# A graph convolution on one core: transposes two groups ahead, and a new order of ScalarE's work

## The chip, the cores and the metric

The kernel runs on one core of a Trainium2 chip. The core has five engines, each with a queue of its own that is worked off in order: TensorE (PE) for matmuls and transposes, VectorE (DVE), ScalarE (ACT), GpSimd (POOL) and SyncE (SP), of which the last two mostly issue DMAs here. Engines wait for each other by semaphores. The metric is the device time of one execution in microseconds (us).

## The reference

One layer of a graph network: 12,500 nodes and 200,000 edges with 64 values each, the edges sorted by their target `dst`.

```python
nodes = x[edge_index].reshape(E, -1)                        # rows of src and dst, side by side
gates = ssp(edge_attr @ We1 + be1) @ We2 + be2              # ssp(x) = softplus(x) - log 2
gates = gates * (1 - sigmoid(5 * (edge_weight - 3.5)))
h     = ssp(nodes @ Wn1 + bn1) @ Wn2 + bn2
sum_  = zeros_like(x).at[dst].add(h * gates)                # messages summed by target
new   = x + ssp(sum_ @ Ws1 + bs1) @ Ws2 + bs2
out   = layernorm(x + new)
```

## The kernel before

**Groups.** The edges are worked in 391 groups of 512 (0 to 390). A group is cut into K = 4 slots of 128 edges. Since the edges are sorted, the targets of half a group lie in a window of W = 42 neighbouring nodes.

**What one group needs, by function.** `gather` (L204) issues on POOL one indirect DMA a slot, which fetches the rows of `src` into a buffer `xg`; the `xg` buffers form a ring of AHEAD + BEHIND. `onehot` (L277, DVE) writes beside these rows which of the 42 targets of the window each edge has. `transposes` (L283, PE) turns the four slots, rows and onehots together, into the PSUM tile `tx`; `xcopy` (L291, ACT) copies that to `xT`. The first layer is made in the PSUM tile `z`: `layer1_bias` (L296), `layer1_edge` (L301) and `layer1_node` (L308), which multiplies `xT` by `wns`: the first 64 rows of `wns` are the weights for `src`, its last 42 the window's rows of a table (nodes times the second half of Wn1, made earlier), which `load` brings by DMA on SP (L216 the edges' values, L224 the window's rows). Softplus is `exps` (L322, ACT), `logs` (L325, ACT) and `softplus` (L330, DVE). The second layer is `layer2_bias` (L347), `layer2_edge` (L354) and `layer2_node` (L359) into `gh`. `hcut` (L368) and `message` (L372) on DVE form the messages, `scatter` (L376, PE) sums them by target into a corner of another group's `z` (it multiplies them by the onehots in `xg`, and is thus the last reader of that buffer), and `window` (L396, DVE) adds that to `sums` at the window's place. The matmuls of L334 are fillers whose result is overwritten.

**Slots made of columns.** For 70 groups one slot isn't gathered from memory: its edges' rows are copied as columns from a copy of x in SBUF, `xh`. That is `columns` (L259): 16 copies on ACT and 8 on DVE in every iteration from 8 on. Their addresses are read into the engine's registers by `read_columns`. Such groups have three gathers and a memset (L202), and `layer1_node` adds two matmuls (L311) for the slot.

**Chunks.** The table is made in 98 chunks of 128 nodes, seven ahead of the loop and one in each of the iterations 0 to 90: `chunk` (L646, PE, into the same `z` as the scatter's sums; it reads x from the storage of `sums`), `keep_chunk` (L649, ACT, to an SBUF tile; every seventh time a DMA writes seven chunks out) and `clear` (L538, DVE).

**Node blocks.** As soon as the sums of 512 nodes are complete, the last layer and the layernorm for them are spread in parts over some iterations (L415 to L475).

**The order is written out by hand.** Python runs the loop for i from −1 to 388; each engine executes its instructions in the order of the program text, and the waits follow from the buffers. In iteration i before the change, cut to what bears on it:

```python
at(gather, i + AHEAD, range(K), [("transposes", i)] if i < BEHIND else ())
layer1_bias(i + 1); layer2_bias(i); scatter(i - 2)
transposes(i + 1); xcopy(i + 1); columns(i, ACT)
layer1_edge(i + 1); chunk(c) or filler; layer1_node(i + 1)
exps(i + 1); logs(i + 1)
keep_chunk(c)                        # c only for i = 0 .. 90
read_columns(i + 1, ACT)
window(i - 2); clear(c)
layer2(i); hcut(i); message(i); softplus(i + 1)
onehot(i + 3); columns(i, DVE)
```

So ACT works copy, columns, exponential, logarithm, chunk, addresses. PE has first layer, second layer, scatter and transposes of different groups in turn. The PSUM tiles `z`, `gh` and `tx` have two buffers each.

Of the kernel before, what the change touches and what calls it, by code (L numbers as in the profile page):

```python
# [31 lines left out]
PIECES = 3  # L32
NB = 512
K = 4
AHEAD = 3
CHUNKS = 7
HEAD = 64
LOADS = 5
SPREADS = 5
PREPARE = 5  # L40
BEHIND = 5
CLOSE = 12


# [60 lines left out]
def gnn_resnorm_kernel(ctx: ExitStack, tc: tile.TileContext, a: dict, out: bass.AP, E: int):  # L105
# [45 lines left out]
    packed, at = {}, 0  # L151
# [94 lines left out]
    def columns(i, queue, pool):  # L246

        count = min(COLUMNS[queue], columns_left(i, queue))
        for j in range(count):
            m, r = divmod(columns_done[queue] + j, P)  # L250
            slot = own[queue][m]
            if r == 0:
                column_tiles[slot] = pool.tile([P, P], F32, name=f"column{queue}", bufs=2)
                side_tiles[slot] = pool.tile([P, P], I32, name=f"side{queue}", bufs=2)
                at = slots.index(slot)
                nc.sync.dma_start(side_tiles[slot], a["sides"][at : at + 1, :].rearrange("o p -> (o p)")
                                  .partition_broadcast(P))
            copy = nc.vector.tensor_copy if queue == 0 else nc.scalar.copy
            copy(column_tiles[slot].bitcast(U8)[:, 4 * r : 4 * r + 4], xh[:, bass.ds(column_at[queue][j] - xh_at, 4)])  # L259
            if r == P - 1:  # L260
                whole.append(slot)
        columns_done[queue] += max(count, 0)
# [17 lines left out]
    def transposes(g, *needs):  # L280
        tx = tx_tile()[:DW].rearrange("f (k e) -> f k e", k=K)
        for k in range(K):
            ins = nc.tensor.transpose(tx[:, k, :], xgs[g][:, k, :DW], ident)  # L283
            if k == 0:
                behind(ins, *needs)
        note(("transposes", g), ins)
        xTs[g] = tx

    def xcopy(g):
        xT = work.tile([DW, K, P], F32, name="xT", bufs=3)  # L290
        note(("xcopy", g), nc.scalar.copy(xT, xTs[g]))  # L291
        xTs[g] = xT.rearrange("f (t h) e -> f h t e", h=2)
# [26 lines left out]
    def exps(g, part=every):  # L319
        if part.start == 0:  # L320
            us[g] = work.tile([P, 3 * HE], F32, name="u")
        nc.scalar.activation(us[g][:, part], z_of(g)[:, part], AF.Exp)  # L322
# [163 lines left out]
    with tc.manual_schedule():  # L486
# [28 lines left out]

        for g in range(AHEAD):
            gather(g)
# [99 lines left out]
        def highest():  # L617
            high = prep.tile([P, NR], F32, name="high")
            nc.vector.tensor_reduce(high, dst_h, AX.X, OP.max)
            nc.vector.tensor_sub(high, high, low)  # L620
            nc.vector.tensor_scalar(high, high, float(1 - W), None, OP.add)
            early = prep.tile([P, NR], F32, name="early")
            nc.vector.tensor_sub(early, least, low)
            nc.vector.tensor_max(high, high, early)
            span = t["span"] = prep.tile([P, 1], F32, name="span")
            nc.vector.tensor_reduce(span, high, AX.X, OP.max)
# [40 lines left out]
        with tc.tile_pool(name="finish", bufs=1) as finish:  # L667
            blocks = list(zip(node_blocks(N), block_steps(N, NG)))
            last = NG - 1
            parts, begun, complete, rest = {}, None, 0, []  # L670

            def at(f, g, *more):
                if 0 <= g < NG:
                    f(g, *more)

            def behind_by(i):
                close = last - CLOSE
                return [g for g in ([i - 2] if i <= close else []) + ([i - 1] if i >= close else []) if g >= 0]

            for g in range(LOADS - 1):  # L680
                load(g)
            for g in range(2):
                onehot(g)
            lowest(1, NR)
            everywhere(1, NR)
            clear(0, CHUNKS)
            highest()
            for i in range(-1, last - 1):
                now = parts.pop(i, [])
                early = [part for part in now if part.tensor]  # L690
                at(load, i + LOADS)
                if i >= 0:
                    at(gather, i + AHEAD, range(K), [("transposes", i)] if i < BEHIND else ())
                layer1_bias(i + 1)
                at(layer2_bias, i)
                for n, g in enumerate(behind_by(i)):
                    scatter(g, zs[i + 1][:, 1, HE + 2 * n * W : HE + 2 * (n + 1) * W])
                transposes(i + 1, ("load", i + 1), ("gather", i + 1), ("onehot", i + 1))
                xcopy(i + 1)
                columns(i, 1, finish)  # L700
                layer1_edge(i + 1)
                c = chunk_of(i, NCH)
                if c is None:
                    busy_before_node(i + 1)
                else:
                    beside_sums = zs[i + 1][:, 1, HE + 2 * W : HE + 2 * W + P]
                    chunk(c, beside_sums)
                layer1_node(i + 1)
                exps(i + 1)
                logs(i + 1)  # L710
                if c is not None:
                    keep_chunk(c, beside_sums)
                read_columns(i + 1, 1)
                for g in behind_by(i):
                    window(g)
                if c is not None:
                    clear(c, c + 1)
                at(busy_before_layer2, i)
                at(layer2, i)
                for part in early:  # L720
                    part.tensor(tx_tile())
                at(hcut, i)
                at(message, i)
                softplus(i + 1)
                for part in early:
                    part.others()
                at(onehot, i + 3)
                read_columns(i, 0)
                columns(i, 0, finish)
                choose(finish)  # L730
                for part in now:
                    if not part.tensor:
                        part.others()
                for action in beside.get(i, []):
                    action()
                complete = i
                if blocks and complete >= blocks[0][1] - PREPARE and not begun:
                    begun = node_block(*blocks[0][0], finish)
                    begun.pop(0).others()
                if blocks and complete >= blocks[0][1]:  # L740
                    steps = next(steps for steps in BLOCK_STEPS if i + steps[-1] < last - 1)
                    for n, part in zip(steps, begun):
                        parts.setdefault(i + n, []).append(part)
                    rest = begun[len(steps) :]
                    blocks.pop(0)
                    begun = None
            assert len(blocks) == 1 and begun and not parts


            begun.pop(2).others()  # L750
            transposes(last, ("load", last), ("gather", last), ("onehot", last))
            xcopy(last)
            layer1_bias(last)
            layer2_bias(last - 1)
            scatter(last - 2, zs[last][:, 1, HE : HE + 2 * W])
            layer1_edge(last)
            layer1_node(last)
            for some in (edge, node):
                exps(last, some)
                logs(last, some)  # L760
            square, variance, root, scale, store = (part.others for part in rest)
            square()
            window(last - 2)
            for g in range(last - 1, last + 1):
                if g not in window_at:
                    window_bases(g)
            layer2(last - 1)
            layer2_bias(last)
            softplus(last, edge)
            layer2_edge(last)  # L770
            softplus(last, node)
            layer2_node(last)
            hcut(last - 1)
            message(last - 1)
            scatter(last - 1, tx_tile()[:, : 2 * W])
            variance()
            root()
            hcut(last)
            message(last)
            scatter(last, tx_tile()[:, : 2 * W])  # L780
            window(last - 1)
            window(last)
            hidden, clamp = begun.pop(0)
            hidden(gh_tile())
            scale()
            clamp()
            store()
            for part in begun:
                node_part(part)
# [162 lines left out]
```

## Time and profile before

| what | us |
|---|---|
| median of 3 runs | 2394.47 (2393.62 to 2402.24) |
| the profiled execution: its time | 2389.88 |
| its span (first to last instruction) | 2388.1 |
| PE busy | 1970.5 (83%) |
| ACT busy | 1511.2 (63%) |
| POOL busy | 1417.0 (59%) |
| DVE busy | 1293.9 (54%) |

The mean granted clock of PE is 0.981. In the lines of the profile that follow, L308 is line 308 of the kernel. A line of the timeline gives start, duration, engine, line, operation, what it writes and reads, and in brackets how long the engine had been idle before it and what ended that. A line of the groups gives busy time, mean ns of one, and idle time with its releasers. Ends of matmuls are modelled. "issue" stands for idle time that no wait in the profile explains.

### The profile page before, as it was taken

What the parts mean: (1) busy time and instruction counts of PE and PEld (TensorE: products, weight loads), DVE (VectorE), ACT (ScalarE), POOL (GpSimd) and SP (SyncE); (2) the same over time, 40 slices, a digit from 0 to 9 for tenths busy, and PEclk for the clock granted to TensorE, in tenths of its full rate; (3) what the DMA queues carried; (4) which work ended last, traced back from release to release, by engine and by line L of the source; (5) the groups of instructions that cost most, each with busy time, mean ns of one, the idle gap of its engine ahead of it and who ended that gap; (6) DMA issues with size and microseconds to landing.
All of it is one profiled execution on the core that took longest, in us unless ns stands there. A gap on an engine that the chain in (4) does not pass through costs nothing.

```text
span 2388.1 us, 48209 instructions
## 1 busy us (share of the span) xinstructions
PE 1970.5 (83%) x12897; PEld 1656.7 (69%) x12897; DVE 1293.9 (54%) x5966; ACT 1511.2 (63%) x7412; POOL 1417.0 (59%) x1497
## 2 busy tenths in 40 slices
PE   6788888888888888888888888888888888888877
PEld 4666677767776776677677667766777767777765
DVE  4355555555555555555555555555555555555544
ACT  3466666666666666666666666666666666666653
POOL 5665665666666666666666666665665666666650
PEclk9799999999999999999999999999999999999988
DMA  6332232322222222222222222222222222222220
GB/s 185 85 91 68 56 75 56 77 61 71 54 57 56 53 59 54 57 56 62 53 59 55 57 58 55 59 59 54 58 58 56 59 57 60 63 57 58 59 50 14
DMA packets 159679, 148.63 MB, mean 62 GB/s; under 512 B 40564, under 2 KB 108949, under 8 KB 159274
## 3 DMA queue, kind: packets, MB, share of 16 engines
q1 hardware_dynamic: 111194, 94.97, 14.4%
q0 software_dynamic: 47776, 49.02, 10.8%
q8 instruction: 109, 1.79, 0.3%
q14 instruction: 166, 1.36, 0.2%
q10 hardware_dynamic: 434, 1.50, 0.2%
HBM read 135.70 MB, written 9.62 MB: 61 GB/s over the span
## 4 chain that ended last, share of the span: by engine, by line
PE 80%; issue 13%; ACT 3%; DVE 2%; another core or an unknown queue 1%; DMA 0%; DVEq 0%; ACTq 0%
PE z L308 18%; PE gh L359 13%; PE z L376 10%; PE tx L283 10%; PE gh L354 7%; PE z L301 6%; PE gh L334 4%; PE gh L347 3%; PE z L296 3%; PE z L334 2%; ACT xT L291 2%; PE tx L415 1%; PE tx L446 1%; PE z L311 1%
## 5 line engine op out<-in xcount | busy, mean ns | idle before, releaser
L204 POOL DMA_INDIRECT xg<-in_x,src_i x1493 | 1416.8, 949 | 919.3 <-PE tx L283 488.8
L308 PE MATMUL z<-xT,wns 106*128 106x256 f32 x1564 | 459.7, 412 | 359.9 <-issue 285.9
L291 ACT COPY xT<-tx 106x512 f32<-106x512 f32 x391 | 229.1, 586 | 779.3 <-PE tx L283 751.1
L259 ACT COPY column<-xh 128x4 uint8 x6016 | 608.7, 193 | 0.0
L308 PEld LDWEIGHTS z<-xT,wns 106*128 106x128 f32 x1564 | 267.8, 193 | 452.4 <-issue 337.7
L368 DVE TENSOR_TENSOR h<-gh,cut 128x256 f32<-128x256 f32 x391 | 165.9, 424 | 747.9 <-PE tx L283 632.2
L359 PE MATMUL gh<-consts,s 128*128 128x64 f32 x3128 | 396.0, 270 | 0.0
L359 PEld LDWEIGHTS gh<-consts,s 128*128 128x128 f32 x3128 | 385.0, 194 | 0.1
L325 ACT ACTIVATE u<-u,one 128x768 f32<-128x768 f32 x392 | 365.8, 933 | 13.4 <-ACT u L322 0.5
L330 DVE SCALAR_TENSOR_TENSOR s<-u,z 128x768 f32<-128x768 f32 x392 | 368.7, 941 | 0.4 <-issue 0.4
L322 ACT ACTIVATE u<-z 128x768 f32<-128x768 f32 x392 | 314.7, 803 | 43.4 <-PE z L308 19.0
L396 DVE TENSOR_TENSOR sums<-sums,z 64x42 f32 x778 | 152.4, 196 | 291.3 <-issue 207.4
L376 PEld LDWEIGHTS z<-xg,msg 128*128 128x128 f32 x1556 | 205.0, 192 | 140.6 <-issue 121.3
L376 PE MATMUL z<-xg,msg 128*128 128x84 f32 x1556 | 265.1, 293 | 15.3 <-DVE msg L372 15.3
L259 DVE COPY column<-xh 128x4 uint8 x2944 | 246.5, 219 | 0.4 <-issue 0.4
L354 PE MATMUL gh<-consts,s 128*128 128x128 f32 x1564 | 243.3, 279 | 1.3 <-DVE s L330 0.8
L283 PE MATMUL tx<-consts,xg 128*106 128x128 f32 x1564 | 238.1, 276 | 0.0
L301 PE MATMUL z<-eT,consts 128*128 128x256 f32 x782 | 237.3, 386 | 0.0
L354 PEld LDWEIGHTS gh<-consts,s 128*128 128x128 f32 x1564 | 210.0, 195 | 2.0 <-DVE s L330 1.1
L283 PEld LDWEIGHTS tx<-consts,xg 128*106 128x106 f32 x1564 | 182.5, 142 | 0.9 <-issue 0.9
L372 DVE TENSOR_TENSOR msg<-gh,h 128x256 f32<-128x256 f32 x391 | 165.8, 424 | 13.4
L334 PEld LDWEIGHTS gh<-consts 128*128 128x128 f32 x778 | 149.5, 195 | 20.5 <-issue 0.3
(109 smaller groups left out, 1456.2 us busy)
## 6 DMA issues: line engine op xcount, KB each, us to landing
eT<-in_eT SPq DMA_DIRECT2D x195, 256.0 KB
xg<-in_x,src_i POOLq DMA_INDIRECT x1493
wns<-table SPq DMA_DIRECT2D x782, 21.0 KB
table<-tb SPq DMA_DIRECT2D x14, 448.0 KB
side<-in_sides SPq DMA_DIRECT2D x70, 64.0 KB
y<-in_x SPq DMA_DIRECT2D x24, 128.0 KB
out<-y SPq DMA_DIRECT2D x24, 128.0 KB
xh<-in_xh SPq DMA_DIRECT2D x2, 781.5 KB
```

The costliest lines, as they stand in the source:

```text
L204: behind(note(("gather", g), nc.gpsimd.indirect_dma_start(out=xg[:, k, :D], out_offset=None, in_=x, in_offset=bass.IndirectOffsetOnAxis(ap ...
L259: copy(column_tiles[slot].bitcast(U8)[:, 4 * r : 4 * r + 4], xh[:, bass.ds(column_at[queue][j] - xh_at, 4)])
L283: ins = nc.tensor.transpose(tx[:, k, :], xgs[g][:, k, :DW], ident)
L301: nc.tensor.matmul(zs[g][:, 0, :HE], we1.rearrange("a h d -> a (h d)"), eTs[g], start=False, stop=True, skip_group_check=True)
L308: nc.tensor.matmul(zn, wns[:, g % REST, h, :], xTs[g][:, h], start=True, stop=not chosen, skip_group_check=True)
L322: nc.scalar.activation(us[g][:, part], z_of(g)[:, part], AF.Exp)
L325: nc.scalar.activation(us[g][:, part], us[g][:, part], AF.Ln, bias=one)
L330: nc.vector.scalar_tensor_tensor(ss[g].rearrange("p i t e -> p (i t e)")[:, part], us[g][:, part], BIG, z_of(g)[:, part], OP.min, OP.max)
L334: nc.tensor.matmul(z, we1.rearrange("a h d -> a (h d)"), ident, start=True, stop=True, skip_group_check=True)
L354: nc.tensor.matmul(v[:, 0, t], ss[g][:, 0, t, :], we2, start=False, stop=False, skip_group_check=True)
L359: nc.tensor.matmul(ghs[g][:, 1, 2 * t + h, :], ss[g][:, 1 + h, t, :], wn2, start=False, stop=h == 1 and t == 1, skip_group_check=True)
L376: ins = nc.tensor.matmul(sc, msgs[g][:, 2 * t : 2 * t + 2, :].rearrange("p h f -> p (h f)"), xgs[g][:, 2 * t : 2 * t + 2, D:DW], start=t = ...
```

## The change

`transposes` and `xcopy` of group i + 2 are issued in iteration i, where those of i + 1 were. Transposes of group 0 and their copy come ahead of the loop, those of the last group go from the epilogue into the loop. For this the onehots are made one group earlier too, and AHEAD is 4 and BEHIND 4 (3 and 5 before). On ACT the copy goes behind the exponential, and the load of the addresses and the columns go behind the logarithm; `keep_chunk` comes behind them. ACT's order is then exponential, copy, logarithm, addresses, columns, chunk.

```diff
-AHEAD = 3
+AHEAD = 4
...
-BEHIND = 5
+BEHIND = 4
...
-            for g in range(2):
+            for g in range(3):
                 onehot(g)
...
             highest()
+            transposes(0, ("gather", 0), ("onehot", 0))
+            xcopy(0)
             for i in range(-1, last - 1):
...
-                    at(gather, i + AHEAD, range(K), [("transposes", i)] if i < BEHIND else ())
+                    at(gather, i + AHEAD, range(K), [("transposes", i + 1)] if i < BEHIND else ())
                 layer1_bias(i + 1)
                 at(layer2_bias, i)
                 for n, g in enumerate(behind_by(i)):
                     scatter(g, zs[i + 1][:, 1, HE + 2 * n * W : HE + 2 * (n + 1) * W])
-                transposes(i + 1, ("load", i + 1), ("gather", i + 1), ("onehot", i + 1))
-                xcopy(i + 1)
-                columns(i, 1, finish)
+                transposes(i + 2, ("load", i + 1), ("gather", i + 2), ("onehot", i + 2))
                 layer1_edge(i + 1)
...
                 layer1_node(i + 1)
                 exps(i + 1)
+                xcopy(i + 2)
                 logs(i + 1)
+                read_columns(i, 1)
+                columns(i, 1, finish)
                 if c is not None:
                     keep_chunk(c, beside_sums)
-                read_columns(i + 1, 1)
                 for g in behind_by(i):
                     window(g)
...
-                at(onehot, i + 3)
+                at(onehot, i + 4)
...
-            transposes(last, ("load", last), ("gather", last), ("onehot", last))
-            xcopy(last)
-            layer1_bias(last)
+            layer1_bias(last, ("load", last))
```

## The prediction

> **What bounds the kernel now.** I read the page's first part (shares), its fifth part (groups and what ended their idle time), then the timeline of one iteration, because the shares name no bound: no engine is full.
>
> ```profile
> PE 1970.5 (83%) x12897; PEld 1656.7 (69%) x12897; DVE 1293.9 (54%) x5966; ACT 1511.2 (63%) x7412; POOL 1417.0 (59%) x1497
> L204 POOL DMA_INDIRECT xg<-in_x,src_i x1493 | 1416.8, 949 | 919.3 <-PE tx L283 488.8
> L308 PE MATMUL z<-xT,wns 106*128 106x256 f32 x1564 | 459.7, 412 | 359.9 <-issue 285.9
> L291 ACT COPY xT<-tx 106x512 f32<-106x512 f32 x391 | 229.1, 586 | 779.3 <-PE tx L283 751.1
> ```
>
> The tempting reading: PE waits 359.9 us ahead of L308 for the copied transposes, and the change makes that copy a group earlier. The timeline says what ends that wait. Here is an iteration with four gathers, then one with three (start, duration, work, idle before it and its releaser; one gather of each is left out).
>
> ```profile
> 1203.69 0.94 POOL L204 DMA_INDIRECT xg<-in_x,src_i  x1 [1.41 <-PE tx L283]
> ...
> 1205.35 0.61 PE L354 MATMUL gh<-consts,s 128*128 128x128 f32 x4
> ...
> 1205.79 1.00 PE L359 MATMUL gh<-consts,s 128*128 128x64 f32 x8
> 1206.19 0.94 POOL L204 DMA_INDIRECT xg<-in_x,src_i  x1 [0.30 <-issue]
> ...
> 1207.15 0.68 PE L376 MATMUL z<-xg,msg 128*128 128x84 f32 x4
> 1207.44 0.94 POOL L204 DMA_INDIRECT xg<-in_x,src_i  x1 [0.30 <-issue]
> ...
> 1208.53 0.39 PE L334 MATMUL z<-consts 128*128 128x128 f32 x2
> 1209.56 0.42 DVE L368 TENSOR_TENSOR h<-gh,cut 128x256 f32<-128x256 f32 x1 [2.79 <-PE tx L283]
> 1209.69 0.59 ACT L291 COPY xT<-tx 106x512 f32<-106x512 f32 x1 [2.40 <-PE tx L283]
> 1209.87 0.94 POOL L204 DMA_INDIRECT xg<-in_x,src_i  x1 [1.49 <-PE tx L283]
> 1210.02 0.42 DVE L372 TENSOR_TENSOR msg<-gh,h 128x256 f32<-128x256 f32 x1
> ...
> 1210.33 1.13 PE L308 MATMUL z<-xT,wns 106*128 106x256 f32 x4 [1.41 <-ACT xT L291]
> 1210.36 0.94 DVE L330 SCALAR_TENSOR_TENSOR s<-u,z 128x768 f32<-128x768 f32 x1
> ...
> 1212.37 0.94 POOL L204 DMA_INDIRECT xg<-in_x,src_i  x1 [0.30 <-issue]
> ...
> 1214.35 0.42 DVE L368 TENSOR_TENSOR h<-gh,cut 128x256 f32<-128x256 f32 x1 [1.41 <-PE z L376]
> ...
> 1214.66 0.94 POOL L204 DMA_INDIRECT xg<-in_x,src_i  x1 [1.35 <-PE tx L283]
> ```
>
> L359, whose result h needs, ends at 1206.79, yet h starts at 1209.56. Then h, the copy and POOL's next train of gathers all start within 0.31 us. That moment is 1209.56 − 1207.44 = 2.12 us after the last gather's start; in the short iteration it is 1214.35 − 1212.37 = 1.98. So while POOL runs its train, what PE has finished becomes visible only about 2.05 us after the train's last gather. Then POOL, which waits on L376 for a free xg buffer, starts the next train. A step from gather to gather is 1.25 (1206.19 to 1207.44). A period is three such steps, 2.12 and 0.31: 6.18 with four gathers (1203.69 to 1209.87), and with one step less 4.79 (1209.87 to 1214.66). The train and PE are in lockstep, and PE's wait for xT is what is left over. Behind the kernel's last gather h starts 0.04 us after L359 ends (2341.77), which speaks for POOL as the cause:
>
> ```profile
> 2335.56 0.95 POOL L204 DMA_INDIRECT xg<-in_x,src_i  x1 [0.30 <-issue]
> ...
> 2339.13 1.13 PE L308 MATMUL z<-xT,wns 106*128 106x256 f32 x4
> 2340.30 0.81 ACT L322 ACTIVATE u<-z 128x768 f32<-128x768 f32 x1 [1.22 <-PE z L308]
> 2340.77 1.00 PE L359 MATMUL gh<-consts,s 128*128 128x64 f32 x8
> 2341.14 0.93 ACT L325 ACTIVATE u<-u,one 128x768 f32<-128x768 f32 x1
> 2341.81 0.42 DVE L368 TENSOR_TENSOR h<-gh,cut 128x256 f32<-128x256 f32 x1 [0.26 <-PE gh L359]
> ```
>
> Why the trace holds PE's results back I can't say; that it will hold them in the changed kernel too is my main assumption.
>
> **The change, part by part.**
>
> *Transposes and copy one group earlier.* No instruction is added: four L283 and one L291 per group as before. What ends: L308 no longer waits for L291, 1.41 us in the iteration above. What is late next: L354, which waits for softplus, behind message, behind h, behind the held L359. From h's release that path is the same before and after: softplus (L330), for which L354 waits, ends at 1211.30, 1.74 us behind it. Nothing in it reads xT, and POOL's train waits on L376, not on L308. So L308 moves into the hole and PE stands the same time ahead of L354. Value in the steady part: 0. From the other side, if the wait for xT does set the pace, PE goes to the 4.79 of the short iteration; that is the first rival.
>
> *Rings and order.* The xg ring keeps 4 + 4 = 8 buffers, so gather g waits for scatter g − 8 as before: POOL's queue is the same, with four gathers more ahead of the loop. Onehots are made three ahead: one more in the prologue, none more in all; transposes of i + 2 wait for a onehot made two iterations earlier: 0. SP's loads aren't moved. At the end the last group's transposes and copy leave its path. They already stood ahead of its bias there, so what goes is at most one L291, 0.59, and PE's transposes, under the 0.70 between L376's end (1207.83) and L334 (1208.53), which holds L301 too; I take −1 (0 to −1.3).
>
> *ScalarE's new order, groups with no chunk.* Per iteration: exponential, copy, logarithm, load of addresses, columns. The spacings are 0.84 (2340.30 to 2341.14), 0.62, 0.93, 0.19 and 1.55 by the rows here and next, 4.13 in sum, under even the short period of 4.79. Window sums (L396) still wait for the exponential alone. Cost: 0.
>
> ```profile
> 484.20 1.62 ACT L259 COPY column<-xh 128x4 uint8 x16
> 485.75 0.81 ACT L322 ACTIVATE u<-z 128x768 f32<-128x768 f32 x1
> 1200.25 0.93 ACT L325 ACTIVATE u<-u,one 128x768 f32<-128x768 f32 x1
> 1201.38 0.42 ACT L454 ACTIVATE y<-y 128x256 f32<-128x256 f32 x1 [0.19 <-issue]
> ```
>
> The columns take 485.75 − 484.20 = 1.55; the load of addresses, which has no row, shows as the 0.19 idle after the logarithm.
>
> *ScalarE's new order, iterations 0 to 90, which carry a table chunk.* Here lies the cost. keep_chunk (L649) stood right behind the logarithm and now stands behind copy, load and columns. DVE's window sums wait for it, the next chunk matmul (L646) waits for the window sums, and PE issues L308 behind L646:
>
> ```profile
> 199.15 0.94 POOL L204 DMA_INDIRECT xg<-in_x,src_i  x1 [2.11 <-PE z L376]
> ...
> 200.38 0.25 ACT L649 COPY tb<-z 128x128 f32<-128x128 f32 x1
> 200.65 0.41 DVE L396 TENSOR_TENSOR sums<-sums,z 64x42 f32 x2 [6.74 <-ACT tb L649]
> ...
> 201.12 0.49 PE L646 MATMUL z<-consts,sums 65*128 65x128 f32 x2 [1.47 <-DVE sums L396]
> ...
> 201.16 0.17 DVE L538 MEMSET sums<- 128x128 f32 x1
> ...
> 201.44 0.60 PE L308 MATMUL z<-xT,wns 106*128 106x256 f32 x2
> ...
> 202.10 0.60 PE L308 MATMUL z<-xT,wns 106*128 106x256 f32 x2
> ...
> 202.73 0.81 ACT L322 ACTIVATE u<-z 128x768 f32<-128x768 f32 x1
> ```
>
> This closes a loop. In the order of the work: L308 to exponential 1.17 (2339.13 to 2340.30), exponential 0.84, copy 0.62, logarithm 0.93, addresses 0.19, columns 1.55, keep 0.27 (200.38 to 200.65), windows 0.47 (to 201.12), L646 0.32 (to L308): 6.36 us. Without copy, addresses and columns it is 4.00, under the train's period: hidden before, binding after. A page of the Trainium skill, "PSUM — Partial Sum Buffer", section "PSUM bank collisions raise a hardware error", says that accesses of ScalarE and VectorE to one bank have to be ordered, reads included; the row [6.74 <-ACT tb L649] agrees, as keep and window read one tile z and neither writes it. By that rule the loop stands, without it this part would cost 0.
>
> The period before in that stretch comes from counting copies in it:
>
> ```profile
> L291 ACT COPY xT<-tx 106x512 f32<-106x512 f32 x83 | 48.7, 586 | 157.1 <-PE tx L283 146.5 <-remote 10.6
> L291 ACT COPY xT<-tx 106x512 f32<-106x512 f32 x279 | 163.5, 586 | 540.1 <-PE tx L283 535.3 <-remote 2.5 <-issue 2.3
> ```
>
> The first is for 100.7 to 593.7: 493.0/83 = 5.94 per group. The second is for 593.7 to 2243: 1649.3/279 = 5.91. Cost: 83 × (6.36 − 5.94) = +35. Bounds: +20 (queueing on ScalarE 0.18 tighter than these rows) to +50 (three groups of 16 have the chosen columns' matmuls among L308's, some 0.4 more, and a train can come late). Before iteration 8 there are no columns, and nothing is charged.
>
> *Sum* against the profiled run, whose time is 2389.88 with a span of 2388.1: +35 − 1 = 2424. The median of the runs is 4.6 above that run, so 2428.
>
> **The rivals.**
>
> *First: the wait for xT sets the pace* (faster). If the hold belongs to PE standing ahead of L308 rather than to POOL's train, it goes with the wait. For it: the copy's 751.1 us of waiting. Against: the release falls at 2.05 behind the train's last gather with four and with three, a PE-made wait would not know that number. Price: 279 × (5.91 − 4.79) = −312, with the chunks' +35: about 2116; loosened in a few groups only, 2350 to 2385. "Perfetto Trace Analysis" of the Trainium skill, section "Optimization Strategy", would have one look at the gaps on the busiest engine and start what ends them sooner, which is this rival; the trace agrees that the gap is there, not that L291 sets its length.
>
> *Second: the chunks' loop is hidden too* (no change). If the loop runs some 0.4 shorter, for instance because the columns overlap their neighbours more than 0.07 us, the time stays: 2390 to 2400. For it: 6.36 is close to the long period of 6.18. Against: short iterations have to grow from 4.79 whatever the long ones do.
>
> *Third: L308 falls into the hold* (much slower). In the new loop L308 ends about 3.2 us behind a train's start, where L359 was held (1206.79 − 1203.69 = 3.1). Were it held until 2.05 behind the last gather, a loop of two periods closes: exponential to windows 4.81 (0.84 + 0.62 + 0.93 + 0.19 + 1.55 + 0.27 + 0.41), clear, h, message, softplus 0.17 + 0.42 + 0.42 + 0.94, L354 to L359's end 1.44, to L376's end 1.04, gather issue 0.31, train and release 5.87: 15.4, so 7.7 a group and 83 × 1.76 = +146: 2540. Decisive point: whether L308's end is seen at once there. The exponential at 202.73 starts 0.03 behind an L308 that ends at 202.70, in a train (from 199.15), 3.55 behind its start, which speaks against it.
>
> **How the numbers follow.** Within 0.5% (12 us) is no change, about what a measurement here can tell. Forecast 0.52, own range 2410 to 2445; third rival 0.11; second 0.13; first 0.24 (0.17 of it at about 2116, 0.07 at 2350 to 2385). A range from 2355 to 2540 holds 0.52 + 0.11 + 0.13 + 0.07 = 0.83. Faster 0.24, same 0.13, slower 0.63.
>
> **What the profile after would show.** Right: L308 no longer waits for L291; trains still 6.1 and 4.8 apart after 594 us, h still 2.05 behind the last gather; up to 594 us L396 waiting for L649, L646 for L396, and periods of 6.3 in all groups. Wrong: h right behind L359 while gathers run, periods near 4.8 (first rival); windows that wait for the exponential early on (second); exponentials that wait 2 us for L308 (third).

## The result, and the profile after

The changed kernel takes 2418.19 us in the median of five runs (2415.08 to 2424.89), the kernel before beside it 2397.71. The ratio is 1.0100, interval 1.0085 to 1.0115: slower by 1%, as forecast (2428, own range 2410 to 2445). The profiled run has a span of 2416.3 us against 2388.1. The sum came out nearly right, but two of its terms were wrong, by 23 and 29 us, in opposite directions.

The start times of h (DVE L368), one a group, cut both spans into stretches. "Half clock" is the time in the stretch at which the trace has PE's clock at one half.

| stretch | before | after | difference | forecast | half clock before, after |
|---|---|---|---|---|---|
| start to group 8 | 103.56 | 95.31 | −8.3 | 0 | |
| groups 8 to 90 (a chunk in each) | 486.4 (5.93 a group) | 498.8 (6.08) | +12.4 | +35 | 17, 24 us |
| groups 90 to 370 | 1656.3 (5.915) | 1685.3 (6.019) | +29.0 | 0 | 10, 327 us |
| groups 370 to 390 | 125.3 | 121.2 | −4.1 | −1 (with the end) | |
| the end | 16.6 | 15.8 | −0.8 | | |

The page of the changed kernel, engines first and then groups (busy, mean ns, idle before and what ended it):

```profile
PE 2135.8 (88%) x12897; PEld 1746.9 (72%) x12897; DVE 1303.8 (54%) x5966; ACT 1455.4 (60%) x7412; POOL 1422.1 (59%) x1497
...
L204 POOL DMA_INDIRECT xg<-in_x,src_i x1493 | 1421.9, 952 | 943.5 <-issue 347.5
L322 ACT ACTIVATE u<-z 128x768 f32<-128x768 f32 x392 | 316.9, 808 | 909.3 <-PE z L308 551.6
...
L308 PE MATMUL z<-xT,wns 106*128 106x256 f32 x1564 | 448.9, 407 | 9.5 <-ACT xT L291 7.7
...
L291 ACT COPY xT<-tx 106x512 f32<-106x512 f32 x391 | 226.1, 578 | 10.0 <-PE gh L565 10.0
```

The change did what it says: PE's idle time ahead of L308 falls from 359.9 to 9.5 us, ScalarE's ahead of the copy from 779.3 to 10.0. Yet the kernel is slower, and POOL's idle time is no less than it was (919.3 before, 943.5). ScalarE now waits ahead of the exponential instead, for L308. PE is "busier" by 165 us with the same 12897 instructions, because they take longer: the windows 600 to 2240 us of the kernel before (first row) and after (second) show the clock (the third value from the end).

```profile
600.00:2240.00 1640.00, 1376.61 (x9160) 1159.88 (x9160) 907.68 (x4269) 1075.08 (x5364) 1002.94 (x1057) 1.00 0.24 57
```

```profile
600.00:2240.00 1640.00, 1483.64 (x8990) 1237.34 (x8990) 898.86 (x4203) 1018.96 (x5275) 988.24 (x1040) 0.90 0.23 56
```

**What the new holes look like.** The timeline of the changed kernel:

```profile
1035.44 1.00 PE L359 MATMUL gh<-consts,s 128*128 128x64 f32 x8
...
1036.80 0.68 PE L376 MATMUL z<-xg,msg 128*128 128x84 f32 x4
...
1038.40 1.03 PE L308 MATMUL z<-xT,wns 106*128 106x256 f32 x4
1038.70 0.94 POOL L204 DMA_INDIRECT xg<-in_x,src_i  x1 [0.30 <-issue]
1040.64 0.42 DVE L368 TENSOR_TENSOR h<-gh,cut 128x256 f32<-128x256 f32 x1 [4.53 <-PE z L308]
1040.85 0.81 ACT L322 ACTIVATE u<-z 128x768 f32<-128x768 f32 x1 [2.46 <-PE z L308]
1040.96 0.94 POOL L204 DMA_INDIRECT xg<-in_x,src_i  x1 [1.32 <-PE z L308]
1041.10 0.42 DVE L372 TENSOR_TENSOR msg<-gh,h 128x256 f32<-128x256 f32 x1
1041.67 0.46 PE L334 MATMUL gh<-consts 128*128 128x128 f32 x2 [2.24 <-DVE msg L372]
...
1044.42 1.15 PE L376 MATMUL z<-xg,msg 128*128 128x84 f32 x4
```

The hold is there: L359 ends at 1036.44, h starts at 1040.64, 1.94 us behind the start of the train's last gather (1038.70). But PE no longer stops ahead of L308 in the meantime. It runs L308 through, its result is held too (ScalarE starts at 1040.85, 1.42 us late), and then PE stands still in one piece, 2.24 us, until message frees the gh tile for L334. Before, L308 waited for the copy and ran behind the release, while DVE made the messages. Between 600 and 2240 us the kernel before has 222 holes (idle times of PE over 0.15 us) ahead of L308, of 1.17 us on average, two over 1.5. The changed one has 97 ahead of L334, 1.19 on average, but 29 over 1.5, 22 over 2 and the longest 3.01. In sum PE idles less there, by the rows above 156 us against 263, since its work takes longer. Behind the hole shown the clock halves; L376 above takes 1.15 in place of 0.68. Windows of 3 us around it:

```profile
1036.00:1039.00 3.00, 3.00 (x21) 2.51 (x21) 0.12 (x1) 2.39 (x18) 2.19 (x3) 1.00 0.34 102
1039.00:1042.00 3.00, 0.76 (x5) 0.33 (x3) 1.32 (x3) 1.15 (x2) 1.58 (x2) 1.00 0.12 29
1042.00:1045.00 3.00, 2.69 (x19) 2.10 (x17) 1.57 (x13) 2.47 (x18) 1.89 (x2) 0.87 0.36 78
1045.00:1048.00 3.00, 3.00 (x13) 2.77 (x13) 2.69 (x12) 0.00 (x0) 1.85 (x2) 0.56 0.41 114
```

PE is busy 0.76 of 3 us, then the clock is 0.87 and 0.56. The stretches at half clock last 3.4, 6.8 or 10.2 us. The Trainium skill, "TensorE: Matmul & The Clock Gate", section "HAM oscillation — how this bites in real kernels", gives as the rule to have no idle gaps over some 3.4 us. Here shorter gaps are enough: none between 600 and 2240 us is longer than 3.01, and 60 stretches begin there at half clock, against 2 before. With 21 of the 22 holes over 2 us the clock halves in the hole or within 3.5 us of its end. But such a hole isn't needed: 33 of the 60 stretches have no hole over 1.5 us in the 10 us ahead of them. Nor does length alone decide: of the holes of 1.0 to 1.5 us, 12 of 14 in the changed kernel were followed by half clock in this way, and none of 182 before. All these stretches begin on one grid of 3.41 us, so where a hole falls may count; what decides is not shown here.

**How that becomes time.** POOL's trains tell it. From a train's last gather to the next train's first the median is 2.36 us, as before (2.38): POOL's side of the lockstep is unchanged. But between groups 90 and 370, 32 trains of the changed kernel come over 2.75 us behind, with 40 us beyond the median in sum, against 11 trains and 9 us before. That difference, 31 us, is about the loss of the stretch. In 26 of the 32 PE had been at half clock for over 1.5 us of the last 7, and in 77 of the 245 other trains too: late trains and half clock go together, which doesn't yet show that the one makes the other.

**The chunk iterations.** The timeline of the changed kernel shows the forecast loop closed:

```profile
364.79 1.03 PE L308 MATMUL z<-xT,wns 106*128 106x256 f32 x4
...
365.86 0.81 ACT L322 ACTIVATE u<-z 128x768 f32<-128x768 f32 x1 [1.89 <-issue]
...
366.56 0.58 ACT L291 COPY xT<-tx 106x512 f32<-106x512 f32 x1
367.03 0.95 ACT L325 ACTIVATE u<-u,one 128x768 f32<-128x768 f32 x1
...
367.87 1.61 ACT L259 COPY column<-xh 128x4 uint8 x16
369.38 0.26 ACT L649 COPY tb<-z 128x128 f32<-128x128 f32 x1
369.67 0.41 DVE L396 TENSOR_TENSOR sums<-sums,z 64x42 f32 x2 [2.40 <-ACT tb L649]
...
370.13 0.49 PE L646 MATMUL z<-consts,sums 65*128 65x128 f32 x2 [0.18 <-DVE sums L396]
...
370.46 1.03 PE L308 MATMUL z<-xT,wns 106*128 106x256 f32 x4
```

Each step waits for the one above it, and from L308 to L308 it is 5.67 us, not 6.36: ScalarE's part from exponential to keep_chunk is 3.52 (365.86 to 369.38) in place of 4.13, since copy and logarithm start 0.70 and 0.47 behind what stands before them and the load of addresses is hidden. From h to h, 16 of the 82 iterations of this stretch took under 5.2 us before and 57 took 6.0 to 6.3. Now none is under 5.66, 33 take 5.66 to 5.75 and 35 take 6.0 to 6.3. So the short iterations grow to the loop's time, and some of the long ones shrink to it.

### The profile page after: what moved, and what is told of

Read it like the earlier page. It is cut to its first block, busy times and chain, and to the rows that moved or that the text cites. A ratio compares the mean times of both kernels' runs of the same rounds, so it can differ in the third digit from the quotient of the medians.

```text
span 2416.3 us, 48318 instructions
## 1 busy us (share of the span) xinstructions
PE 2135.8 (88%) x12897; PEld 1746.9 (72%) x12897; DVE 1303.8 (54%) x5966; ACT 1455.4 (60%) x7412; POOL 1422.1 (59%) x1497
## 4 chain that ended last, share of the span: by engine, by line
PE 60%; DVE 12%; ACT 8%; another core or an unknown queue 6%; issue 6%; DVEq 4%; ACTq 1%; DMA 1%; POOL 0%; POOLq 0%
PE z L308 11%; PE gh L359 11%; PE z L376 9%; PE gh L354 7%; PE tx L283 5%; PE z L301 5%; DVEq L242 4%; ACT column L259 3%; DVE s L330 3%; DVE h L368 3%; PE gh L347 3%; PE z L296 2%; PE z L334 2%; ACT u L322 2%
## 5 line engine op out<-in xcount | busy, mean ns | idle before, releaser
L204 POOL DMA_INDIRECT xg<-in_x,src_i x1493 | 1421.9, 952 | 943.5 <-issue 347.5
L368 DVE TENSOR_TENSOR h<-gh,cut 128x256 f32<-128x256 f32 x391 | 166.0, 425 | 588.8 <-PE z L308 166.6
L308 PE MATMUL z<-xT,wns 106*128 106x256 f32 x1564 | 448.9, 407 | 9.5 <-ACT xT L291 7.7
L359 PE MATMUL gh<-consts,s 128*128 128x64 f32 x3128 | 410.0, 276 | 0.0
L359 PEld LDWEIGHTS gh<-consts,s 128*128 128x128 f32 x3128 | 399.4, 200 | 0.1
L376 PEld LDWEIGHTS z<-xg,msg 128*128 128x128 f32 x1556 | 226.9, 210 | 145.8 <-issue 131.8
L354 PE MATMUL gh<-consts,s 128*128 128x128 f32 x1564 | 274.3, 300 | 60.9 <-DVE s L330 48.6
L308 PEld LDWEIGHTS z<-xT,wns 106*128 106x128 f32 x1564 | 291.2, 210 | 34.3 <-ACT xT L291 8.2
L376 PE MATMUL z<-xg,msg 128*128 128x84 f32 x1556 | 291.1, 314 | 10.1 <-DVE msg L372 8.8
L354 PEld LDWEIGHTS gh<-consts,s 128*128 128x128 f32 x1564 | 216.2, 200 | 103.7 <-DVE s L330 80.9
L334 PEld LDWEIGHTS gh<-consts 128*128 128x128 f32 x778 | 139.6, 200 | 195.7 <-PE z L308 120.1
L334 PE MATMUL gh<-consts 128*128 128x128 f32 x778 | 169.5, 300 | 122.0 <-DVE msg L372 75.9
L283 PE MATMUL tx<-consts,xg 128*106 128x128 f32 x1564 | 266.1, 299 | 4.8 <-ACT u L322 4.8
L259 DVE COPY column<-xh 128x4 uint8 x2944 | 267.4, 197 | 2.4 <-issue 1.9
L301 PE MATMUL z<-eT,consts 128*128 128x256 f32 x782 | 264.9, 424 | 1.0 <-issue 1.0
L283 PEld LDWEIGHTS tx<-consts,xg 128*106 128x106 f32 x1564 | 206.3, 156 | 6.2 <-ACT u L322 5.0
```

What stands on the lines that cost most here:

```text
L204: behind(note(("gather", g), nc.gpsimd.indirect_dma_start(out=xg[:, k, :D], out_offset=None, in_=x, in_offset=bass.IndirectOffsetOnAxis(ap ...
L301: nc.tensor.matmul(zs[g][:, 0, :HE], we1.rearrange("a h d -> a (h d)"), eTs[g], start=False, stop=True, skip_group_check=True)
L308: nc.tensor.matmul(zn, wns[:, g % REST, h, :], xTs[g][:, h], start=True, stop=not chosen, skip_group_check=True)
L334: nc.tensor.matmul(z, we1.rearrange("a h d -> a (h d)"), ident, start=True, stop=True, skip_group_check=True)
L354: nc.tensor.matmul(v[:, 0, t], ss[g][:, 0, t, :], we2, start=False, stop=False, skip_group_check=True)
L359: nc.tensor.matmul(ghs[g][:, 1, 2 * t + h, :], ss[g][:, 1 + h, t, :], wn2, start=False, stop=h == 1 and t == 1, skip_group_check=True)
```

## The experiments

Each run was compared with the kernel before on the same chip. That kernel took 2396 and 2366 us in some of these comparisons and 1993 in the others: there the hold is absent, and the kernel is bound by something else (below). Each verdict says which it was.

**keep_chunk back in its place** (hold; before 2395.67).

```diff
                 logs(i + 1)
+                if c is not None:
+                    keep_chunk(c, beside_sums)
                 read_columns(i, 1)
                 columns(i, 1, finish)
-                if c is not None:
-                    keep_chunk(c, beside_sums)
```

> The changed kernel with keep_chunk back right behind the logarithm, ahead of the addresses and columns; the rest as changed. Theory K (the chunk iterations lose because keep_chunk stands behind the columns): iterations 8 to 90 go back from 6.08 us a group to about 5.93, that is -12, and the whole to about 2405; the stretch behind iteration 90 stays at 6.02 with the clock of PE near 0.91. Rival (the copy between exponential and logarithm delays the chunk iterations, keep_chunk's place is harmless): no change, 2418.

Measured: 2411.08 (2400.68 to 2424.51), ratio 1.0065 (1.0035 to 1.0095). The chunk stretch is 6.05 us a group, not 5.93: a miss. The loop is gone (short iterations of 4 to 4.8 us are back), but half clock in the stretch rises from 24 to 99 us. It seems that without the loop the chunk iterations lose in the way that the later ones do; no run separates the two. So this run didn't settle the place of keep_chunk.

**Transposes ahead alone** (hold; beside the same runs). ScalarE as before: `xcopy(i + 2)` and `columns(i, 1)` right behind `transposes(i + 2)`, then exponential, logarithm, keep_chunk, `read_columns(i + 1, 1)`.

> Transposes and their copy two groups ahead, but ScalarE's order as before: copy, columns, exponential, logarithm, keep_chunk, addresses. Theory C (PE no longer waits ahead of L308, its idle time is bunched into fewer and longer holes ahead of L334, and in these the clock of PE is halved; this comes with the transposes' place alone): mean clock about 0.91 to 0.92, 6.0 us a group behind iteration 90, and about 2405 because keep_chunk is in its old place. Rival O (ScalarE's order makes the loss behind iteration 90): clock back at 0.98, 5.91 us a group, 2385 or less.

Measured: 2407.27, ratio 1.0047 (1.0034 to 1.0060). Clock 0.929, half clock 196 us between groups 90 and 370, 5.99 us a group there: theory C.

**The order alone** (hold; beside the same runs).

```diff
                 xcopy(i + 1)
-                columns(i, 1, finish)
...
                 logs(i + 1)
+                read_columns(i, 1)
+                columns(i, 1, finish)
                 if c is not None:
                     keep_chunk(c, beside_sums)
-                read_columns(i + 1, 1)
```

> ScalarE's order alone: exponential, logarithm, addresses, columns, keep_chunk, with the transposes and their copy where they were before (the copy ahead of the exponential). Theory C: PE still waits ahead of L308 in every group, the clock stays at 0.98 and the stretch behind iteration 90 at 5.91; the chunk iterations pay for keep_chunk: 2400 to 2412. Rival O: the stretch behind iteration 90 loses its 0.1 us a group here, with a lower clock: 2430 or more.

Measured: 2398.26, ratio 1.0016 (0.9995 to 1.0037). Half clock 17 us, 5.926 us a group behind 90; the chunk stretch 6.05, with 5.6 to 5.7 in the short iterations. PE's rows for 600 to 2240 us, this kernel first, the transposes-ahead kernel second:

```profile
600.00:2240.00 1640.00, 1372.61 (x9136) 1157.77 (x9134) 911.38 (x4259) 1115.11 (x5360) 1002.13 (x1054) 0.99 0.25 57
```

```profile
600.00:2240.00 1640.00, 1461.39 (x9053) 1197.20 (x9051) 902.26 (x4223) 1062.68 (x5300) 987.12 (x1046) 0.94 0.24 57
```

So the lower clock and the loss behind group 90 come with the transposes' place; the chunks' loss comes with the order (6.05 us a group, against 5.97 with the transposes' place alone and 5.93 before). The transposes' place alone costs 0.5%. The order alone costs 0.2%, which isn't clear of the noise; the two together cost 1.0%.

**Fillers in the holes** (hold; beside the same runs).

```diff
+    def fill(g, n):
+        opened_tx[g] = tx_tile()
+        for _ in range(n):
+            busy(opened_tx[g][:, :P])
...
+                if c is None and i >= 0 and not early and i + 3 <= last:
+                    fill(i + 3, 3)
                 at(busy_before_layer2, i)
```

`transposes` takes the opened tile.

> The changed kernel with three more filler matmuls (128 columns, about 0.22 us each) behind L308 in the iterations behind 90 without a block part; they write the tx buffer of the next transposes, which is free, so they run in the hole ahead of L334 and change no result. Theory C: PE is busy in the holes, the clock is halved far less often (0.97 or more), and the stretch behind iteration 90 falls from 6.02 to 5.9 us a group or less: 2390 or less in spite of 0.66 us more work a group. Rival (the lower clock is a symptom, PE has slack enough for it): no gain, 2418 to 2440.

Measured: 2429.20, ratio 1.0138 (1.0118 to 1.0157): a miss in time, not in the clock. The profiled run is at 0.971, half clock 61 us in place of 327, and the excess of late trains falls from 40 to 23 us. But the median from a train's last gather to the next train rises from 2.36 to 2.42, 0.06 for each of some 280 trains, 16 us. The stretch takes 6.01 us a group, as good as unchanged, and 12 of its 20 late trains don't have that much half clock ahead of them. Perhaps the extra 0.66 us of PE a group costs what the clock gains; perhaps the clock made little of the loss. That the clock makes the 29 us is therefore not shown; what is shown is that it can be kept up, at no profit by this means.

**Two gathers a group, kernel before.** In `gather`, `if k >= 2 or padding(g, k) or ...`. First run (no hold; before 1993.19):

> The kernel before with two gathers a group instead of four; the other two slots are set to zero on DVE, so their edges' source rows are missing from the result. Theory P (the train of gathers on POOL sets the period: steps of 1.25, then 2.05 until PE's results are seen, then 0.31): the train needs 0.31 + 1.25 + 2.05 = 3.6 us, under PE's own 4.8, so the period behind iteration 90 falls from 5.91 to 4.8 to 5.3 us and h starts at once behind L359: about 2050 to 2200. Rival (PE's wait for xT, or something else on PE, DVE or ScalarE sets it): the period stays near 5.9 and the time near 2390.

Measured: 1992.82, as the kernel before with four. Where there is no hold the train doesn't set the period. Second run (hold; before 2366.33):

> The kernel before with two gathers a group instead of four, the other two slots set to zero. On a chip with the hold, theory P (train of gathers sets the period) gives 4.8 to 5.3 us a group behind iteration 90 and 2050 to 2200 in all; the rival (the hold does not depend on the train's length) 5.9 us and 2390. On a chip without the hold: 1993 as in the earlier run, the same as the kernel before.

Measured: 2001.14, ratio 0.8455 (0.8424 to 0.8486), 4.96 us a group behind 90. The timeline of this run:

```profile
1002.60 0.95 POOL L204 DMA_INDIRECT xg<-in_x,src_i  x1 [0.30 <-issue]
1003.82 1.00 PE L359 MATMUL gh<-consts,s 128*128 128x64 f32 x8
1004.86 0.42 DVE L368 TENSOR_TENSOR h<-gh,cut 128x256 f32<-128x256 f32 x1
1006.13 0.95 POOL L204 DMA_INDIRECT xg<-in_x,src_i  x1 [2.58 <-PE z L376]
```

The release point, 2.05 behind the last gather, would be 1004.65, before L359 ends; h starts at once, and POOL waits 2.58 us for the scatter. Shortening the train takes 365 us off the kernel before. One might object that the hold was absent from this execution. It was there: where L359 ends within 1 us of the last gather, h is held in four of five groups behind 600 us, by 0.57 to 1.69 us, and in the first run of the same kernel, without the hold, by 0.04 to 0.47 in the same four groups. One of them, first here and then in the first run:

```profile
1650.96 1.00 PE L359 MATMUL gh<-consts,s 128*128 128x64 f32 x8
1651.20 0.94 POOL L204 DMA_INDIRECT xg<-in_x,src_i  x1 [0.30 <-issue]
1652.77 0.42 DVE L368 TENSOR_TENSOR h<-gh,cut 128x256 f32<-128x256 f32 x1 [0.83 <-PE gh L359]
```

```profile
1641.77 1.00 PE L359 MATMUL gh<-consts,s 128*128 128x64 f32 x8
1642.02 0.95 POOL L204 DMA_INDIRECT xg<-in_x,src_i  x1 [0.30 <-issue]
1642.81 0.42 DVE L368 TENSOR_TENSOR h<-gh,cut 128x256 f32<-128x256 f32 x1
```

Such groups are few: a train of two is over before most results of PE are due. So the train, together with the hold, set the period, as the prediction's main assumption has it. The release falls 1.57 us behind the last gather here, not 2.05.

**Two gathers, changed kernel** (no hold; before 1993.19).

> The same cut to two gathers in the changed kernel. Theory P: with POOL out of the way the wait ahead of L308 is what the transposes two groups ahead take away, so this is faster than the kernel before with two gathers, by 0.1 to 0.5 us a group behind iteration 90 (30 to 140 us in all). Rival (the change is worth nothing even then): the two are within 10 us.

Measured: 1979.09, ratio 0.9927 (0.9907 to 0.9947). Behind group 90 it is 4.67 us a group against 4.96, 82 us less; in the chunk stretch 5.81 against 4.96, 70 us more. The change pays behind group 90 once neither train nor hold covers it, and its loss in the chunk stretch eats most of that.

**The same with keep_chunk right behind the logarithm** (no hold; before 1993.47).

> The changed kernel with two gathers a group (the other slots zero) and keep_chunk right behind the logarithm, to test keep_chunk's place where no train and no hold covers it. The changed kernel with two gathers took 5.81 us a group in the chunk iterations and 4.67 behind, 1979 in all; the kernel before with two gathers 4.96 in both, 1993. Theory K (the loop through keep_chunk, columns and L646 makes the 5.81): 4.6 to 5.0 in the chunk iterations, 1880 to 1915 in all. Rival (the copy between exponential and logarithm, or the columns' place, makes it): 5.6 to 5.8 and 1965 to 1985.

Measured: 1899.72, ratio 0.9540 (0.9518 to 0.9563); the chunk stretch goes from 5.81 to 4.88, behind 90 it stays at 4.67. This settles what the first run left: the loop through keep_chunk is real.

**Columns behind the logarithm, keep_chunk ahead of them, in the kernel before** (no hold; before 1993.19): as in the order alone, with `keep_chunk` first.

> The kernel before with ScalarE's columns and their addresses moved behind the logarithm, but behind keep_chunk too. Theory K: with keep_chunk in its place right behind the logarithm the chunk iterations stay at 5.93 us a group (6.05 in the run with the order alone), so 2385 to 2397. Rival (the columns' place itself costs the chunk iterations 0.1 us a group): 2398 to 2408.

Measured: 2183.87, ratio 1.0959 (1.0940 to 1.0977), 5.4 to 5.5 us a group everywhere, for a reason of which neither theory had thought. Its timeline:

```profile
1002.96 0.57 ACT L291 COPY xT<-tx 106x512 f32<-106x512 f32 x1
...
1003.59 1.13 PE L308 MATMUL z<-xT,wns 106*128 106x256 f32 x4 [0.50 <-ACT xT L291]
...
1004.76 0.81 ACT L322 ACTIVATE u<-z 128x768 f32<-128x768 f32 x1 [1.22 <-PE z L308]
...
1005.60 0.93 ACT L325 ACTIVATE u<-u,one 128x768 f32<-128x768 f32 x1
...
1006.71 1.62 ACT L259 COPY column<-xh 128x4 uint8 x16 [0.18 <-issue]
...
1008.24 0.57 ACT L291 COPY xT<-tx 106x512 f32<-106x512 f32 x1
```

The next group's copy stands behind the columns, and L308 waits for the copy: copy to copy is 5.28 us. In the changed kernel the copy is a group ahead, so its order doesn't close this loop: there the two halves of the change belong together. With the hold the period of 6.1 is longer than this loop (order alone, +0.2%).

**POOL waits on DVE instead of PE.**

```diff
-        [("transposes", i)] if i < BEHIND else ()
+        [("transposes", i)] if i < BEHIND else [("hcut", i + AHEAD - 6)]
```

> The kernel before; the first gather of a group waits for DVE's h of six groups before (which itself waited for the scatter in question) instead of for the scatter on PE. It asks what holds PE's results back. Theory P1 (they are held while gathers run and POOL's next one waits on PE): h starts at once behind L359 and the period falls under 5.5. Theory P2 (they are held by running gathers, whatever POOL waits for): the period stays at 5.9 and the time at 2390 to 2400.

> The kernel before with the first gather of a group waiting for DVE's h of six groups before instead of for the scatter on PE, once more, as the earlier run of it fell on a chip without the hold. On a chip with the hold (kernel before near 2370 to 2395): theory P1 (results are held while gathers run and POOL's next one waits on PE): h starts at once behind L359, period under 5.5, time under 2250. Theory P2 (held by running gathers, whatever POOL waits for): 2360 to 2400, as the kernel before. On a chip without the hold: 1993 again.

Measured: 1992.62 (a single run) and 1994.02, beside 1993.19 and 1993.47. Both fell where the hold is absent, so they can't tell P1 from P2. They show that absence: in the second run h starts 0.04 behind L359 in the middle of POOL's gathers.

```profile
1002.66 0.94 POOL L204 DMA_INDIRECT xg<-in_x,src_i  x1 [0.31 <-issue]
1002.90 1.00 PE L359 MATMUL gh<-consts,s 128*128 128x64 f32 x8
1003.91 0.95 POOL L204 DMA_INDIRECT xg<-in_x,src_i  x1 [0.30 <-issue]
1003.94 0.43 DVE L368 TENSOR_TENSOR h<-gh,cut 128x256 f32<-128x256 f32 x1
```

**The changed kernel again** (hold; before 2366.33).

> The changed kernel once more, because the chip of the last four runs showed the kernel before at 1993 us in place of 2395, with h right behind L359 and no hold. If this chip has the hold (kernel before near 2395): again about 1.0% slower. If it has none (kernel before near 1993): the chunk iterations bound by keep_chunk's loop at 5.7 to 5.8 us a group against 4.96, +65, and behind iteration 90 about 4.67 against 4.96, -80, as in the two-gather runs: 1970 to 1985, 0.5 to 1% faster. Rival (the change is worth nothing behind iteration 90 without the hold either): 2050 or more there.

Measured: 2383.08, ratio 1.0074 (1.0050 to 1.0097), half clock 267 us between groups 90 and 370, and 5.90 us a group there. In this comparison the kernel before was 31 us faster than beside the first result, and no profile of it was kept; so where the 17 us of loss lie can't be told. With four gathers and no hold the changed kernel was not timed; the two-gather runs are the nearest to it.

## Why the prediction was right, point by point

- *The train of gathers and the hold set the pace.* Right where it was predicted: the median from last gather to next train is 2.36 after, 2.38 before, and two gathers take 15% off. But h 2.05 behind the last gather, the sign of a steady lockstep, held only in part: between groups 90 and 370 h starts 1.85 to 2.2 us behind a gather in 272 of 280 groups before, in 139 after; in 113 it now starts within 1.3 us of one. The hold itself stays unexplained, and in part of the comparisons it wasn't there.
- *Value of the earlier transposes in the steady part: 0.* Wrong: +29 us. The step that failed is "L308 moves into the hole and PE stands the same time ahead of L354". PE does stand there, ahead of the filler L334, but unevenly: some holes of 2 to 3 us, 60 stretches at half clock in place of 2, and 32 late trains in place of 11. I had priced idle time without asking how it is spread, and the clock not at all. That the loss comes with the transposes' place is shown by the runs of each part alone. That the halved clock makes the late trains is not shown: 26 of the 32 have it ahead of them, but the fillers restored the clock without restoring the time, so the cause of the 29 us stays open.
- *ScalarE's new order without a chunk: 0.* Right by the order alone (5.926 us a group behind 90, against 5.915).
- *The chunk iterations: +35.* The mechanism was right, link by link, and was shown by 5.81 to 4.88 us a group with two gathers; the term was mis-sized: a loop of 5.67, not 6.36, so +12. I had added spacings taken between other neighbours, and the copy's 0.62 stands in no row that I showed. On ScalarE the steps overlap more (0.61 us over the five). The loop doesn't set the period in all groups either, as the sum had it: 35 of 82 iterations still take 6.0 to 6.3.
- *The end: −1, the rest 0.* The last 20 groups gained 4.1 us. The first eight gained 8.3, which the sum didn't have; the profile gives no single cause, and both kernels are irregular there.
- *The rivals.* The first (PE's wait sets the pace) is refuted with the hold, by the change itself: the wait fell by 350 us, the time didn't. With two gathers and no hold it is true in kind, with 0.29 us a group (4.96 to 4.67) in place of 1.12. The second (chunk loop hidden) had its condition right, a loop shorter by 0.7, but not its outcome: no iteration is under 5.66, as was said against it. The third (L308 falls into the hold) happens, as at 1040.85, but behind iteration 90 rather than in the chunk loop, and in some groups, not in all.

The total of 2428 against 2418 is thus partly luck: −23 in one term, +29 in another, and −12 at the start and the end, which the sum had at −1.

## What to carry to other kernels

Before a wait is taken away, look at what ended it: if that is a resource which would release its results at the same moment anyway, the wait moves, and what counts is whether the new place is worse. Idle time of PE has a shape as well as a sum: 263 us of it, nearly all in even holes ahead of one line, kept the full clock; 156 us, spread unevenly and ahead of another line, didn't. And a clock that falls is no proof of what the time is lost to: the fillers brought it back and gained nothing. On an in-order queue a short copy that another engine needs (keep_chunk, the transposes' copy) must not stand behind long work that nobody waits for; price such a loop by spacings between the same neighbours.

## What the runs showed of the hardware that I had not expected

The kernel before took 2366 to 2398 us in the median of some comparisons and 1993 in others, each time steadily (1989.02 to 1997.83 in the latter). The median from L359's end to h is 2.64 us in its profile with the hold; the variants without it have 0.04. It isn't a matter of the chip's number: chip 3 showed the hold beside the first four experiments, and none half an hour later, where the kernel before took 1993.47. What brings the hold about was not found: the length of the train decides what it costs where it exists, and the run that would have told whether POOL's wait on PE matters did not meet it.

PE's clock halves for 3.4, 6.8 or 10.2 us, beginning on a grid of 3.41 us, with 21 of 22 holes of 2 to 3 us, but also where no hole over 1.5 us stands ahead (33 of 60). That was enough to bring the mean clock of 600 to 2240 us from 1.00 to 0.90.

The edit of ScalarE's order cost 0.2% (at most 0.4%) with the hold, and a near relative of it 9.6% without: a change measured under one bound says little about the other.
